# The first two rows of a macaron block: second row five chunks behind, its norm spread over chunks, weight tiles turned in other places, terms of h two chunks ahead

## The chip, the cores and the metric

The kernel runs on one core of a Trainium2 chip. The metric is the device time of one execution in microseconds; the time before is the median of three runs.

## The reference

Eight rows of 512 tokens with 512 channels go through a feed-forward layer, a sliding-window attention and a second feed-forward layer with the same weights. Only the first layer matters here. Its weights are quantised on the way in, to groups of 64 with one scale:

```
w = w_fp32.astype(bfloat16);  w_g = w.reshape(-1, 64)
scale = clip(mean(abs(w_g)), 1e-8)
w_hat = clip(round(w_g / scale), -1, 1) * scale
xn = layernorm(x)
gate, up = split(xn @ w_hat_gate_up.T)          # 2048 each
h = silu(gate) * up
x = x + 0.5 * (h * rsqrt(mean(h*h) + eps)) @ w_hat_proj.T
```

## The kernel before

A stage of the feed-forward layer (`ffn_stage`) handles one row (512 tokens) after the other. The 2048 hidden channels are cut into FC = 16 chunks of 128. For a chunk, TensorE (PE) makes gate and up with 8 matmuls each (`gate_or_up`), since x is held as a high and a low term over 4 blocks of channels; ScalarE (ACT) makes silu of gate; VectorE (DVE) multiplies it with up (`product`); ACT copies h as its high term (`high_term`), DVE makes the low term (`low_term`), and PE projects the chunk with 8 matmuls (`project`) into four accumulators, LAG = 2 chunks later. The sum of h squared per token, which scales the output at the end (`finish`), comes from a matmul with a column of ones.

The first two rows (`first_rows`) run together, because the weights are quantised while they are used. The order on PE, DVE and ACT is written out by hand; GpSimd (POOL) and the DMA queue of SP take their part where the dependencies let them. A `Quantised` tile is one chunk of gate and up weights (g, 16 of them) or two chunks of projection weights (pr, 8 of them). It goes through these steps: load (SP), magnitude and sign (ACT), scales (DVE), spread of the scales over the groups (ACT), five operations in two halves (DVE), and `turned`: eight PE transposes into PSUM, a copy by ACT into the weight tile, and a store of that tile for the last stage. The weight tile g[c+1] is quantised during chunk c.

In the loop over c, row 0 is at chunk c and row 1 at chunk d = c - LAG. Row 0 is normed ahead of the loop; the statistics of row 1 come all at the end of chunk 0, and its scaling and transposes (`normed`) all at the end of chunk 1. Row 1's h is squared, summed on DVE (sumsq) and stored in DRAM (h_kept), because PSUM holds the accumulators of one row only. After the loop it is loaded back (`back`), its terms are made again and it is projected, while the norm of row 2 runs between the chunks (`spread_norm`). The rest of the rows run one at a time.

What a PSUM pool holds matters for the order. Gate and up share two buffers: gate of one row takes the buffer that the gate before it left when its silu had been read, and up the one that the product before it freed. The transposes of the norm and of the weights share two buffers of `ps_tr`, and one of these holds the sums of squares of row 0 (`ms_first`) all along. The terms of h (hs) have three buffers, the pool `work` for silu, h, squares and back has five.

In one chunk before, PE issues gate and up of row 0, the turning of g[c+1], gate and up of row 1, the sums of row 0's squares, in even chunks the turning of pr[u-1], and the projection of chunk c - 2. ACT's order has magnitude and sign of g[c+2] ahead of silu of row 0, then the copy of the turned weights, the high term and the square.

Of the kernel before, what the change touches and what calls it, by code (L numbers as in the profile page):

```python
# [24 lines left out]
def macaron_block(  # L25
# [34 lines left out]
    nc.vector.tensor_copy(ident16, ident)  # L60
    ones = const.tile([P, 1], F32, name="ones")
    nc.vector.memset(ones, 1.0)
    mhalf = const.tile([P, TB], F32, name="mhalf")
    nc.vector.memset(mhalf, -0.5)

# [46 lines left out]
    class Quantised:  # L112
# [20 lines left out]
            self.wf = self.stage.tile(self.shape, F32, tag="wf", name=f"wf_{self.name}", bufs=2)  # L133
            nc.sync.dma_start(self.wf, self.src)

        def magnitude_and_sign(self):

            self.mag = self.bf16(f"mag_{self.kind}", self.ahead)
            nc.scalar.activation(self.mag, self.wf, AF.Abs)
            self.sgn = self.bf16(f"sgn_{self.kind}", self.ahead)  # L140
            nc.scalar.activation(self.sgn, self.wf, AF.Sign)

# [46 lines left out]


    def inv_sqrt(dst, src):
        nc.gpsimd.tensor_tensor(dst, src, mhalf, ALU.pow)

    def norm(xnpool, xspool, psum, tag, xt, split, name):

        if split:
            xs = xspool.tile([P, 2, DC, T], F32R, tag="xs", name=f"xs_{name}")
        else:  # L200
            xs = xspool.tile([P, DC, T], F32, tag="xs", name=f"xs_{name}")
        mv = small.tile([P, TB, 2], F32, tag="mv", name=f"mv_{name}")
        rstd = small.tile([P, TB], F32, tag="nrstd", name=f"rstd_{name}")

        def statistics(t):
            st = small.tile([P, 6], F32, tag="st", name=f"st_{name}_{t}")
            nc.vector.bn_stats(st, xt[:, t, :])
            nc.vector.bn_aggr(mv[:, t, :], st)
            if t == TB - 1:
                var = small.tile([P, TB], F32, tag="nvar", name=f"var_{name}")  # L210
                nc.vector.tensor_scalar(var, mv[:, :, 1], LN_EPS, None, ALU.add)
                inv_sqrt(rstd, var)

        xns = {}

        def scaled(t):
            xns[t] = xnpool.tile([P, D], F32, tag="xn", name=f"xn_{name}_{t}")
            nc.vector.tensor_scalar(
                xns[t], xt[:, t, :], mv[:, t, 0:1], rstd[:, t : t + 1], ALU.subtract, ALU.mult
            )  # L220

        def transposed(t):
            xn = xns.pop(t)
            pt = psum.tile([P, DC, P], F32, tag=tag, name=f"ptn_{name}_{t}")
            for c in range(DC):
                nc.tensor.transpose(pt[:, c, :], xn[:, c * P : (c + 1) * P], ident)  # L226
            cols = slice(t * P, (t + 1) * P)
            if split:
                nc.scalar.copy(xs[:, 0, :, cols], pt)  # L229
                nc.vector.tensor_tensor(  # L230
                    xs[:, 1, :, cols], pt, xs[:, 0, :, cols].bitcast(F32), ALU.subtract
                )
            else:
                nc.scalar.copy(xs[:, :, cols], pt)

        return xs, statistics, scaled, transposed


    LAG = 2

    def ffn_stage(kind, source, target, first):
# [26 lines left out]
        def row_loaded(b):  # L268
            xts[b] = xpool.tile([P, TB, D], F32, tag="x", name=f"x_{kind}{b}")
            for t in range(TB) if first and b == 0 else [slice(None)]:  # L270
                nc.sync.dma_start(xts[b][:, t], source(b)[:, t])
            xss[b], *norms[b] = norm(
                xnpool, xspools[b % 2], ps_tr, "tr", xts[b], True, f"{kind}{b}"
            )

        def gate_or_up(b, c, i):
# [12 lines left out]
        def silu(b, c, gate):  # L289
            sg = work_tile("sg", b, c)  # L290
            nc.scalar.activation(sg, gate, AF.Silu)  # L291
            return sg
# [11 lines left out]
        def low_term(h, hs):  # L304
            nc.vector.tensor_tensor(hs[:, 1, :], h, hs[:, 0, :].bitcast(F32), ALU.subtract)  # L305
# [6 lines left out]
        def project(ops, e, hs):  # L312
            for t in range(TB):
                for part in range(2):
                    nc.tensor.matmul(  # L315
                        ops[t], hs[:, part, t * P : (t + 1) * P], wp[e // 2][:, e % 2, :],
                        start=(e == 0 and part == 0), stop=(e == FC - 1 and part == 1),
                    )
# [36 lines left out]
        def first_rows():  # L355


            own = ExitStack()
            ms = ps_tr.tile([P, TB], F32, tag="tr", name="ms_first")
            stage = own.enter_context(tc.tile_pool(name="stage", bufs=1))  # L360
# [11 lines left out]
            waiting = list(order)  # L372

            def begun(tile_):
                tile_.magnitude_and_sign()
                if waiting:
                    waiting.pop(0).load()

            def normed(b, t):

                if t < TB:
                    norms[b][1](t)
                if t >= 1:
                    norms[b][2](t - 1)
# [22 lines left out]
            ops = outputs(0)  # L407
            sumsq = work.tile([P, T], F32, tag="ss", name="ss_second", bufs=1)
            hs, square = {}, None
            for c in range(FC + LAG):  # L410
                u, odd, d = c // 2, c % 2 == 1, c - LAG
                if c < FC:
                    gate0 = gate_or_up(0, c, 0)
                    up0 = gate_or_up(0, c, 1)
                    if c + 2 < FC:
                        begun(g[c + 2])
                    sg0 = silu(0, c, gate0)
                    if c + 1 < FC:
                        g[c + 1].first_half()
                        g[c + 1].second_half()  # L420
                    h0 = product(0, c, up0, sg0)
                    if c + 1 < FC:
                        g[c + 1].turned()
                    hs[c] = high_term(0, c, h0)
                    if odd:
                        pr[u].first_half()
                    else:
                        pr[u].scales()
                if c == FC + 1:
                    project(ops, d, hs.pop(d))  # L430
                if d >= 0:
                    gate1 = gate_or_up(1, d, 0)
                    up1 = gate_or_up(1, d, 1)
                if c < FC:
                    low_term(h0, hs[c])
                    sq0 = work_tile("sq", 0, c)
                    nc.scalar.activation(sq0, h0, AF.Square)
                    if c + 2 < FC:
                        g[c + 2].scales()
                if d >= 0:  # L440
                    sg1 = silu(1, d, gate1)
                if c < FC:
                    if not odd:
                        pr[u].spread()
                    if c + 2 < FC:
                        g[c + 2].spread()
                if c == FC + 1:
                    finish(0, ops, ms)
                if d >= 0:
                    h1 = product(1, d, up1, sg1)  # L450
                    nc.sync.dma_start(h_kept[d], h1)

                    square = sumsq if d == 0 else work_tile("sq", 1, d)
                    nc.scalar.activation(square, h1, AF.Square)
                if c < FC:
                    if odd:
                        pr[u].second_half()
                        if u + 1 < FC // 2:
                            begun(pr[u + 1])
                    for t in range(TB):  # L460
                        nc.tensor.matmul(
                            ms[:, t : t + 1], sq0[:, t * P : (t + 1) * P], ones,
                            start=(c == 0 and t == 0), stop=(c == FC - 1 and t == TB - 1),
                        )
                if c == 0:
                    for t in range(TB):
                        norms[1][0](t)
                if c == 1:
                    for t in range(TB + 1):
                        normed(1, t)  # L470
                if not odd and u:
                    pr[u - 1].turned()
                if 0 <= d < FC - 1:
                    project(ops, d, hs.pop(d))
                if d >= 1:
                    nc.vector.tensor_tensor(sumsq, sumsq, square, ALU.add)


            ms = sums_of(1, sumsq)
            ops = outputs(1)  # L480
            kept = {}
            for e in range(-2, FC):
                if e + 2 < FC:
                    kept[e + 2] = work_tile("back", 1, e + 2)
                    nc.sync.dma_start(kept[e + 2], h_kept[e + 2])
                if e >= 0:
                    ht = high_term(1, e, kept[e])
                    low_term(kept.pop(e), ht)
                    project(ops, e, ht)
                if e == 1:  # L490
                    stored(0)
                spread_norm(2, e, 2)
            finish(1, ops, ms)
            own.close()
# [370 lines left out]
```

## Time and profile before

| what | value |
|---|---|
| median of three runs | 2529.14 us (2523.03 to 2530.17) |
| profiled execution | 2521.33 us, span 2519.4 us |
| mean granted TensorE clock | 0.986 |
| PE busy | 2421.2 us, 96% of the span |
| DVE busy | 1323.8 us, 53% |
| ACT busy | 983.2 us, 39% |
| POOL busy | 908.9 us, 36% |
| first gate matmul of row 0, chunk 0 | 24.48 us |
| first projection of row 1 | 242.60 us |
| last projection matmul of row 1 | ends at 284.70 us |

The busy shares are means over the whole span. The change touches the first 285 us alone, so the numbers of that stage are what to read: the busy time by stretch, the timeline of a chunk, and on each line of it the idle time before an instruction, with the instruction that ended it. The span runs from the first to the last instruction; the profiled execution is 1.9 us longer than its span.

### The profile page before, as it was taken

What the parts mean: (1) busy time and instruction counts of PE and PEld (TensorE: products, weight loads), DVE (VectorE), ACT (ScalarE), POOL (GpSimd) and SP (SyncE); (2) the same over time, 40 slices, a digit from 0 to 9 for tenths busy, and PEclk for the clock granted to TensorE, in tenths of its full rate; (3) what the DMA queues carried; (4) which work ended last, traced back from release to release, by engine and by line L of the source; (5) the groups of instructions that cost most, each with busy time, mean ns of one, the idle gap of its engine ahead of it and who ended that gap; (6) DMA issues with size and microseconds to landing.
All of it is one profiled execution on the core that took longest, in us unless ns stands there. A gap on an engine that the chain in (4) does not pass through costs nothing.

```text
span 2519.4 us, 40507 instructions
## 1 busy us (share of the span) xinstructions
PE 2421.2 (96%) x16184; PEld 1772.3 (70%) x16184; DVE 1323.8 (53%) x3800; ACT 983.2 (39%) x1476; POOL 908.9 (36%) x775
## 2 busy tenths in 40 slices
PE   4998999999999999999999999997999999999998
PEld 3777788888888455555555555554688888888887
DVE  6785444444443566666666666665334444443442
ACT  5773222222222256555555555556222222222221
POOL 0000244445445133333333333333245444444444
PEclk8999999999999999999999999999999999999999
DMA  3443200000011100011010000022300000000000
GB/s 134 154 152 117 79 1 34 34 34 1 34 68 51 51 1 27 18 39 35 23 35 18 23 18 23 18 101 85 125 13 22 34 34 1 34 34 1 34 17 17
DMA packets 43564, 111.65 MB, mean 44 GB/s; under 512 B 3440, under 2 KB 7536, under 8 KB 40304
## 3 DMA queue, kind: packets, MB, share of 16 engines
q1 hardware_dynamic: 33392, 83.90, 9.4%
q10 hardware_dynamic: 9984, 25.17, 3.0%
q8 instruction: 127, 2.08, 0.4%
q14 instruction: 61, 0.50, 0.1%
HBM read 67.11 MB, written 41.94 MB: 43 GB/s over the span
## 4 chain that ended last, share of the span: by engine, by line
PE 89%; DVE 5%; ACT 3%; DMA 1%; issue 1%; POOL 0%; SPq 0%; POOLq 0%; DVEq 0%; ACTq 0%
PE gu_c L280 19%; PE gu_a L280 17%; PE o_c L315 9%; PE o_a L315 8%; PE sm L651 5%; PE sp L683 5%; PE wk L597 5%; PE av L719 5%; PE wq L597 4%; PE wo L597 4%; PE wv L597 4%; PE abT L737 1%; PE neg L669 1%; PE ptn_a L226 1%; PE ptn_b L226 1%
## 5 line engine op out<-in xcount | busy, mean ns | idle before, releaser
L280 PE MATMUL gu_a<-xs_a,wgu_a 128*128 128x512 f32 x2048 | 494.7, 395 | 1.8 <-ACT wgu_a L176 1.1
L280 PE MATMUL gu_c<-xs_c,wgu_c 128*128 128x512 f32 x2048 | 491.1, 393 | 0.7 <-ACT xs_c L229 0.7
L703 POOL TENSOR_SCALAR_AFFINE_SELECT pT<-pT 128x1024 f32<-128x1024 f32 x224 | 242.3, 1102 | 592.1 <-ACT pT L698 592.1
L280 PEld LDWEIGHTS gu_a<-xs_a,wgu_a 128*128 128x128 f32 x2048 | 385.5, 190 | 82.1 <-ACT wgu_a L176 1.4
L280 PEld LDWEIGHTS gu_c<-xs_c,wgu_c 128*128 128x128 f32 x2048 | 383.6, 189 | 80.0 <-ACT xs_c L229 0.9
L660 DVE CUSTOM_DVE_ANT_0 seen<-sm,window 128x256 f32<-128x256 f32 (+1 forms) x1024 | 331.2, 388 | 142.5 <-PE sm L651 142.0
L315 PE MATMUL o_a<-wp_a,hs_a 128*128 128x512 f32 x1024 | 257.1, 396 | 17.0 <-ACT wp_a L176 10.5
L315 PE MATMUL o_c<-wp_c,hs_c 128*128 128x512 f32 x1024 | 251.5, 389 | 0.0
L517 POOL TENSOR_TENSOR sq_c<-h_c 128x512 f32<-128x512 f32 x120 | 125.0, 1042 | 316.0 <-DVE h_c L296 302.5
L296 DVE TENSOR_TENSOR h_c<-gu_c,sg_c 128x512 f32<-128x512 f32 x128 | 88.3, 690 | 281.5 <-PE gu_c L280 280.2
L315 PEld LDWEIGHTS o_a<-wp_a,hs_a 128*128 128x128 f32 x1024 | 192.6, 190 | 60.7 <-ACT wp_a L176 11.9
L696 ACT ACTIVATE pT<-sp 128x512 f32<-128x512 f32 (+1 forms) x384 | 181.2, 547 | 127.7 <-PE sp L683 127.7
L698 ACT ACTIVATE pT<-pT 128x2048 f32<-128x2048 f32 (+1 forms) x128 | 217.3, 1698 | 8.4 <-DVE pT L692 4.4
L315 PEld LDWEIGHTS o_c<-wp_c,hs_c 128*128 128x128 f32 x1024 | 192.2, 188 | 39.9
L296 DVE TENSOR_TENSOR h_a<-gu_a,sg_a 128x512 f32<-128x512 f32 x128 | 88.3, 690 | 239.4 <-PE gu_a L280 233.8
L518 POOL TENSOR_TENSOR ss_c<-ss_c,sq_c 128x512 f32<-128x512 f32 x120 | 192.2, 1602 | 8.9
L291 ACT ACTIVATE sg_c<-gu_c 128x512 f32<-128x512 f32 x128 | 76.6, 599 | 265.1 <-PE gu_c L280 249.5
L301 ACT CAST hs_c<-h_c 128x512 fp32r<-128x512 f32 x128 | 79.4, 621 | 250.0 <-DVE h_c L296 250.0
L517 POOL TENSOR_TENSOR sq_a<-h_a 128x512 f32<-128x512 f32 x90 | 94.2, 1047 | 228.8 <-DVE h_a L296 218.8
L305 DVE TENSOR_TENSOR hs_c<-h_c,hs_c 128x512 fp32r<-128x512 f32 x128 | 124.0, 969 | 83.2 <-ACT hs_c L301 83.2
L291 ACT ACTIVATE sg_a<-gu_a 128x512 f32<-128x512 f32 x128 | 76.4, 597 | 228.3 <-PE gu_a L280 219.3
L651 PE MATMUL sm<-k,q 32*128 32x256 f32 (+1 forms) x2048 | 147.5, 375 | 2.5 <-DVE negs L660 2.0
(135 smaller groups left out, 3019.1 us busy)
## 6 DMA issues: line engine op xcount, KB each, us to landing
wf_gu<-w_gate_up_dram SPq DMA_DIRECT2D x16, 512.0 KB, 3.5
wgu_kept<-wgu_a SPq DMA_DIRECT2D x16, 512.0 KB, 2.6
rows_a<-x_a ACTq DMA_DIRECT2D x8, 1024.0 KB, 3.9
x_b<-rows_a SPq DMA_DIRECT2D x8, 1024.0 KB, 4.9
xr<-rows_a ACTq DMA_DIRECT2D x32, 256.0 KB, 3.1
rows_b<-xr SPq DMA_DIRECT2D x32, 256.0 KB, 2.4
x_c<-rows_b SPq DMA_DIRECT2D x8, 1024.0 KB, 4.8
wgu_c<-wgu_kept SPq DMA_DIRECT2D x16, 512.0 KB, 6.6
```

Source lines behind the costliest of these rows:

```text
L280: nc.tensor.matmul(ps, wgu[c][:, i * DC + k, :], xss[b][:, part, k, :], start=(k == 0 and part == 0), stop=(k == DC - 1 and part == 1),)
L291: nc.scalar.activation(sg, gate, AF.Silu)
L296: nc.vector.tensor_tensor(h, up, sg, ALU.mult)
L315: nc.tensor.matmul(ops[t], hs[:, part, t * P : (t + 1) * P], wp[e // 2][:, e % 2, :], start=(e == 0 and part == 0), stop=(e == FC - 1 and ...
L517: nc.gpsimd.tensor_tensor(sq, h, h, ALU.mult)
L518: nc.gpsimd.tensor_tensor(sumsq, sumsq, sq, ALU.add)
L597: nc.tensor.matmul(ps, lhs, rhs, start=(n == 0), stop=(n == len(pairs) - 1))
L651: nc.tensor.matmul(tiles[g][:, h, : n * P], qs[i][h][r, t * P : (t + 1) * P], ks[i][r, at], start=True, stop=True,)
L660: nc.vector.tensor_tensor_reduce(out=seen[:, : n * P], in0=tiles[g][:, h, : n * P], in1=window[:, (2 - n) * P :], scale=-1.0, scalar=3.4e3 ...
L696: nc.scalar.activation(under, tiles[g][:, :, : n * P], AF.Relu, scale=-1.0)
L698: nc.scalar.activation(seen, seen, AF.Exp, scale=-1.0)
L703: nc.gpsimd.affine_select(out=half, in_=half, compare_op=ALU.is_ge, fill=0.0, base=0, pattern=[[0, 2 * NG], [sign, P]], channel_multiplier ...
```

## The change

Row 1 runs `BEHIND = TB + 1` = 5 chunks behind row 0 instead of 2, so the loop has 21 turns instead of 18. The norm of row 1 is spread: one block of statistics in each of the chunks 0 to 3, each with its own power on POOL (`each=True`), and one block of scaling and transposes in each of the chunks 1 to 4. The turning of g[c+1] moves behind gate and up of row 1, that of pr[u-1] between gate and up of row 1. The sign of g[c+2] comes after the silu of row 0. The projection of row 0 stays two chunks behind. After the loop, the loads of h run four chunks ahead instead of two, both terms of h are made two chunks ahead of the projection, and the sums of row 1 (`sums_of`) come after its second projected chunk. One activation with Silu is put at the very start, so that its table is the first one loaded.

```
+    nc.scalar.activation(const.tile([P, 1], F32, name="begin"), ones, AF.Silu)
...
+            if each or t == TB - 1:
+                which = slice(t if each else 0, t + 1)
+                var = small.tile([P, TB], F32, tag="nvar", name=f"var_{name}_{t}")
+                nc.vector.tensor_scalar(var[:, which], mv[:, which, 1], LN_EPS, None, ALU.add)
+                inv_sqrt(rstd[:, which], var[:, which])
...
+            BEHIND = TB + 1
...
-            for c in range(FC + LAG):
-                u, odd, d = c // 2, c % 2 == 1, c - LAG
+            for c in range(FC + BEHIND):
+                u, odd, d = c // 2, c % 2 == 1, c - BEHIND
...
                     if c + 2 < FC:
-                        begun(g[c + 2])
+                        g[c + 2].magnitude()
                     sg0 = silu(0, c, gate0)
+                    if c + 2 < FC:
+                        signed(g[c + 2])
...
                     h0 = product(0, c, up0, sg0)
-                    if c + 1 < FC:
-                        g[c + 1].turned()
                     hs[c] = high_term(0, c, h0)
...
                 if d >= 0:
                     gate1 = gate_or_up(1, d, 0)
+                if not odd and 0 < u <= FC // 2:
+                    pr[u - 1].turned()
+                if d >= 0:
                     up1 = gate_or_up(1, d, 1)
                 if c < FC:
+                    if c + 1 < FC:
+                        g[c + 1].turned()
                     low_term(h0, hs[c])
                     sq0 = work_tile("sq", 0, c)
                     nc.scalar.activation(sq0, h0, AF.Square)
...
-                if c == 0:
-                    for t in range(TB):
-                        norms[1][0](t)
-                if c == 1:
-                    for t in range(TB + 1):
-                        normed(1, t)
-                if not odd and u:
-                    pr[u - 1].turned()
-                if 0 <= d < FC - 1:
-                    project(ops, d, hs.pop(d))
+                if c < TB:
+                    norms[1][0](c)
+                if 1 <= c <= TB:
+                    norms[1][1](c - 1)
+                    norms[1][2](c - 1)
+                if 0 <= c - LAG < FC:
+                    project(ops, c - LAG, hs.pop(c - LAG))
+                if c == FC + LAG:
+                    finish(0, ops, ms)
...
-            ms = sums_of(1, sumsq)
             ops = outputs(1)
-            kept = {}
-            for e in range(-2, FC):
-                if e + 2 < FC:
-                    kept[e + 2] = work_tile("back", 1, e + 2)
-                    nc.sync.dma_start(kept[e + 2], h_kept[e + 2])
+            kept, terms = {}, {}
+            for e in range(-4, FC):
+                if e + 4 < FC:
+                    kept[e + 4] = work_tile("back", 1, e + 4)
+                    nc.sync.dma_start(kept[e + 4], h_kept[e + 4])
+                if 0 <= e + 2 < FC:
+                    terms[e + 2] = high_term(1, e + 2, kept[e + 2])
+                    low_term(kept.pop(e + 2), terms[e + 2])
                 if e >= 0:
-                    ht = high_term(1, e, kept[e])
-                    low_term(kept.pop(e), ht)
-                    project(ops, e, ht)
+                    project(ops, e, terms.pop(e))
                 if e == 1:
                     stored(0)
+                    ms = sums_of(1, sumsq)
```

## The prediction

> **What bounds the kernel now.** I read the page first, then the busy time of each engine by stretch, then the timeline of the stretches that the change touches, and last the order in which the two built programs issue on each engine. That order is the same from row 2 on, so only the first 284 us can differ. From the page:
>
> ```profile
> span 2519.4 us, 40507 instructions
> ...
> PE   4998999999999999999999999997999999999998
> ...
> PEclk8999999999999999999999999999999999999999
> ```
>
> A digit is 63 us. PE is under 90% in four slices, and two of them, the first (4) and the fourth (8, 189 to 252 us), lie in the first rows: that is where PE stands idle. The stretches below follow the start of row 0's gate matmul by chunk (chunk 0 at 24.5, 1 at 34.0, 2 at 57.0, 5 at 95.2, 15 at 214.2), then row 1's second projection from 242.6 to 283.8. Columns: PE, PEld, DVE, ACT and POOL busy, granted clock, DMA share.
>
> ```profile
> 24.50:34.00 9.50, 6.69 (x33) 5.33 (x33) 6.22 (x10) 9.33 (x11) 0.00 (x0) 1.00 0.62 216
> 34.00:57.00 23.00, 12.10 (x51) 9.21 (x50) 17.21 (x32) 10.42 (x14) 1.38 (x1) 0.66 0.20 71
> 57.00:71.90 14.90, 13.63 (x67) 11.05 (x66) 11.95 (x18) 10.96 (x14) 0.00 (x0) 0.84 0.33 123
> ...
> 95.20:118.70 23.50, 21.91 (x121) 17.92 (x120) 18.94 (x30) 16.89 (x22) 0.00 (x0) 1.00 0.46 157
> ...
> 214.20:242.60 28.40, 22.91 (x114) 18.57 (x112) 11.53 (x20) 6.88 (x11) 1.01 (x1) 1.00 0.20 70
> 242.60:283.80 41.20, 35.37 (x145) 26.95 (x146) 18.44 (x34) 11.27 (x19) 2.39 (x2) 0.96 0.40 139
> ```
>
> Chunk 1 (34 to 57) loses 11 us of PE to row 1's norm, the second projection 6. A pair of full chunks (23.5 us) loses only 1.6: 0.36 before the even chunk's turning of its weights and 1.23 before its projection, which waits for the copy of wp. So there is little to win in the full chunks, and something at both ends. Two places of the timeline carry the argument. Chunk 1:
>
> ```profile
> 41.91 0.62 PE L175 MATMUL ptq_gu<-ident,q_wt_gu 128*128 128x128 bf16 x8 [2.40 <-DVE q_wt_gu L168]
> ...
> 42.56 1.01 ACT L176 CAST wgu_a<-ptq_gu 128x1024 fp32r<-128x1024 bf16 x1 [3.97 <-PE ptq_gu L175]
> ...
> 43.47 0.62 ACT L301 CAST hs_a<-h_a 128x512 fp32r<-128x512 f32 x1
> ...
> 43.99 0.63 ACT L437 ACTIVATE sq_a<-h_a 128x512 f32<-128x512 f32 x1
> ...
> 44.67 1.86 PE L461 MATMUL ms_first<-ones,sq_a 128*128 128x1 f32 x8 [2.15 <-ACT sq_a L437]
> ```
>
> Where no row-1 matmul stands between the turning (ptq_gu) and the sums (ms_first), PE waits until ACT has copied the turned weights and squared h. In full chunks gate and up of row 1 stand there and hide it. The second place is the second projection, one of its last four chunks:
>
> ```profile
> 273.25 0.49 PE L315 MATMUL o_a<-wp_a,hs_a 128*128 128x512 f32 x1 [1.19 <-ACT hs_a L301]
> ...
> 274.06 1.89 PE L315 MATMUL o_a<-wp_a,hs_a 128*128 128x512 f32 x7 [0.31 <-DVE hs_a L305]
> ```
>
> The terms of h are made in the chunk that uses them, behind the copy of the next row's norm, and PE waits for both.
>
> **What the Trainium skill says.** "TensorE: Matmul & The Clock Gate", section "What's actually happening": the PE clock falls to half after one idle window of a free-running 3.4 us and returns after a busy one. The trace agrees: the clock reads 0.50 from 164 to 167 us, and the projection there takes 3.59 instead of 2.11 us. That followed 2.65 us of ms_first, ptq_p and a wait, not a whole window of idleness. The same page's table (row on queue depth) has ScalarE and VectorE as strict FIFO; the trace agrees, as sq_a waits behind wgu_a at 42.56 above. "ScalarE: Activation LUTs", section "What ACT_TABLE_LOAD costs": about 1283 ns a load; the trace shows two in this stage, 1.28 us each (0.78 and 29.19).
>
> **The change part by part.** Times are of the profiled execution.
>
> 1. Start. The Silu table is loaded at 0.8 in place of the first set, so the load at 29.19 goes; up0 of chunk 0 ends at 29.8, so this frees 1.3 us of ACT but at most 0.7 of the path. DVE's seven small constant operations (7.84 to 8.57) now stand behind qsum of g[0] instead of in a wait: +0.7 to everything up to gate0 of chunk 0. Together 0: chunk 1 begins at 34.1.
>
> 2. Chunks 1 to 4, row 0 alone. Each now carries a quarter of row 1's norm. Statistics 0.95 and scaling 0.5 stand last on DVE, and PE meets the norm's transposes (ptn) before its projection and the next gate. The chain of one chunk is therefore serial. Odd: after up0, DVE does h 0.6, half of p 1.35, low term 0.6, scales 1.35, second half of p 1.95, statistics and scaling 1.45 = 7.3; then ptn 1.1 and projection. Even: h 0.7, hs 0.6, copy of wp 0.95, ptq_gu 0.6, copy of wgu 1.0, square 0.6, ms 0.9, ptn 1.0 and projection. One buffer of ps_tr is held by ms_first, so ptq_gu waits for the copy of wp, and that copy is on the path. After such gaps PE starts cold: gate and up take 5.4 (as at 34.0) or, after a cold projection of 3.4, about 4.3. Chunk by chunk: 14.1 (no projection yet), 15.1, 16.4, 13.3. Gate0 of chunk 5 then starts at 93.0 against 95.2, but row 1 is three chunks further behind. POOL's four powers of 1.0 to 1.4 us replace one; scaling uses the power of the chunk before, so they are hidden. The statistics hold up nothing else on DVE that is late, except xn, which is counted.
>
> 3. Chunks 5 to 14, both rows. PE now issues gate0, up0, gate1, (ptq_p), up1, ptq_gu, ms, projection. The wait for wp goes (ptq_p lies before up1: 1.8 us cover the copy) and the wait for q_wt goes. But sq0 stands on ACT behind the copy of wgu, which waits for ptq_gu, and ms follows ptq_gu at once. The lost time is 0.04 + 0.91 + 0.63 + 0.05 = 1.63 us in every chunk, from the rows above without hs. PE per odd chunk: 3.63 + 3.75 + 0.62 + 1.63 + 0.81 + 1.96 = 12.4; even with ptq_p 0.43: 12.8. A pair is 25.2 against 23.5. Nobody else is later: DVE's quantising of 3.4 us ends 0.5 to 3 us before ptq_gu, h0 comes 0.7 us before up1 needs its PSUM buffer, product h1 ends before the next up0. Loads and stores on SP keep their chunk, a store of h by three chunks later. Five pairs: 126. Clock drops: the stretch of ptq, wait and ms is 3.05 us, now in each chunk; before, seven of 2.65 us gave one drop of 1.5 us. I take two, +3, bounds 0 and 15. Chunk 15 starts at 93.0 + 126 + 3 = 222.0 against 214.2.
>
> 4. The end of row 1. Five chunks of row 1 are left instead of two. Chunk 15: 10.15, 16: 6.0, 17: 5.6, 18: 3.65. Then finish(0) lies on DVE between two products: h 0.7, var, POOL's power and half 1.6, four x_a 2.73, sum and h of chunk 14 1.3, so up1 of chunk 15 starts 6.35 after up1 of 13 and ends at 8.2 (0.9 late). From there to the first projection 4.5 as before (238.1 to 242.6: product, store issue 0.4, load of back 2.7, hs). 38.1 against 28.4; projection starts at 260.1 against 242.6.
>
> 5. Second projection. Before: 16 x 1.81 = 29.0, four transposes 2.4, cold start 1.6, one wait 0.6, and four chunks of 4.3 instead of 2.4 (7.6): 41.2. With terms two ahead the 7.6 goes: hs has three buffers, a term needs 1.4 us and has 3.6. ms (0.8) moves in from before it. rows_a is now issued behind hs of chunk 3, so x of row 2 lands some 14 us after the first projection (6.3 + 5.5 us as before) and DVE's statistics, with two low terms behind them, hold PE about 0.5. SP issues the load ahead of back 10 and later, which is early enough. Sum 34.3; the stage ends at 294.4.
>
> Against 283.8 (284.7 less 0.9 of gate work that PE had done early) this is **+10.6 us**. The profiled execution took 2521.3 (span 2519.4 and 1.9 around it), which gives 2531.9. The median of the runs shown, 2529.1, lies 7.8 above that execution, so I put the change on the median: 2539.7. Some 0.3%, 7.6 us, is about what a measurement of this kernel can tell from no change.
>
> **Rivals.**
> Faster: chunks 1 to 4 run at DVE's busy time, not at the serial chain. DVE has 11.4 us in an odd and 9.4 in an even one, so 10.3 on average; the four take 41 instead of 59, and with no clock drop the sum is 10.6 - 18 - 3 = -10: 2519 to 2521. For it: chunk 0 took 9.5. Against it: chunk 0 has no ptn and no projection. It decides if chunks 1 to 4 average below 10.5 us.
> Even: PE is warm there (4 us less) and no clock drops in full chunks (3 less): +3.6, 2533. For it: six of seven stretches before kept the clock.
> Slower still: each wait of 1.63 drops the clock: ten times 1.5 instead of 3, +22, 2552.
> The terms ahead do nothing, since hs buffers free too late: +7.6, 2547. Against it, the ring: a buffer is free two projections before it is needed.
>
> **How the numbers follow.** Forecast 0.48, even 0.26, faster 0.12, slower still 0.09, no gain in the terms 0.05. The forecast's own range is 2532 to 2548 (clock 0 to 4 drops, early chunks 5 either way); the whole one reaches to both edges, 2521 to 2552. Faster 0.12, same 0.27, slower 0.61.
>
> **What would show it.** Right: ms_first waiting about 1.6 us for sq_a some fifteen times; full pairs at 25.2; gate0 of chunk 5 near 93 and of chunk 15 near 222; the projections after 260 with no wait for hs_a. Wrong: pairs at or below 23.5, chunks 1 to 4 at 10 us, or a second projection near 41.

## The result and the profile after

The kernel after takes 2546.91 us (median of five runs, 2542.35 to 2548.10) against 2523.67 us of the kernel before on the same chip: a ratio of 1.0082, with a 95% interval of 1.0061 to 1.0103. It is slower by 23 us; the forecast was slower by 10.6. Its profiled execution took 2547.95 us with a span of 2546.1 us, that of before 2521.33 and 2519.4 us. From the page of after:

```profile
span 2546.1 us, 40511 instructions
...
PE   4889999999999999999999999998899999999998
...
PEclk9889999999999999999999999999899999999999
```

The second and the third slice (64 to 191 us) are now 8 in both rows, where before they were 9. They lie mostly in the full chunks, where the kernel before lost little. (The 8s further on are in code that the change doesn't touch.) The busy time by stretch says it in microseconds. The columns are the stretch, its length, busy time of PE, PE's weight loads, DVE, ACT and POOL, the granted clock, and the DMA share with GB/s. The stretches are chunks 1 to 4, chunks 5 to 14, the tail (from gate of row 0, chunk 15, to the first projection of row 1) and the second projection:

```profile
35.80:95.40 59.60, 40.47 (x186) 33.21 (x186) 42.62 (x74) 34.14 (x42) 2.89 (x4) 0.74 0.30 111
95.40:234.60 139.20, 122.89 (x602) 98.98 (x601) 90.75 (x140) 81.51 (x106) 0.00 (x0) 0.90 0.34 121
234.60:272.80 38.20, 32.78 (x153) 26.46 (x151) 15.46 (x25) 10.47 (x17) 1.01 (x1) 1.00 0.20 72
272.80:306.50 33.70, 33.65 (x152) 27.55 (x153) 18.64 (x34) 11.47 (x19) 1.57 (x2) 0.95 0.52 168
```

Against before:

| stretch | before | forecast | after |
|---|---|---|---|
| gate0 of chunk 1 starts | 34.0 | 34.1 | 35.8 |
| chunks 1 to 4 | 61.2 | 58.9 | 59.6 |
| chunks 5 to 14 | 119.0 | 129 | 139.1 |
| tail | 28.4 | 38.1 | 38.3 |
| second projection | 41.2 | 34.3 | 33.7 |
| end of the first rows | 283.8 | 294.4 | 306.6 |

In chunks 5 to 14 PE is idle for 16 us, which is ten waits of 1.63, and the clock is 0.90 where before it was 0.99. The waits of PE in the first rows (total, times, longest):

```profile
PE ms_first L474 <- ACT sq_a L452: 26.6, 15, 2.5
...
PE o_a L322 <- ACT hs_a L308: 4.7, 1, 4.7
...
PE gu_a L287 <- DVE h_a L303: 0.7, 1, 0.7
```

One full chunk of after in the timeline (start, duration, what, and in brackets the idle time before it with what ended it):

```profile
184.92 0.62 PE L179 MATMUL ptq_gu<-ident,q_wt_gu 128*128 128x128 bf16 x8
...
185.58 1.01 ACT L180 CAST wgu_a<-ptq_gu 128x1024 fp32r<-128x1024 bf16 x1 [2.67 <-PE ptq_gu L179]
186.49 0.63 ACT L452 ACTIVATE sq_a<-h_a 128x512 f32<-128x512 f32 x1
...
187.17 1.54 PE L474 MATMUL ms_first<-ones,sq_a 128*128 128x1 f32 x8 [1.63 <-ACT sq_a L452]
...
188.58 3.76 PE L322 MATMUL o_a<-wp_a,hs_a 128*128 128x512 f32 x8
```

The square of h stands on ACT behind the copy of the turned weights (186.49 behind 185.58), ms_first waits 1.63 us for it, and the projection behind it runs at half clock: 3.76 us, where a chunk that kept the clock shows 2.10. Seven of the ten chunks lost it. The rest of the span is 2239.5 us against 2235.6. Its instructions are the same, and in the profiled executions of all the kernels below it lies between 2234 and 2240 us, so these 3.9 us are no more than executions differ by and are not put down to the change.

### The profile page after: what moved, and what is told of

Its sections match the earlier page's. It is cut to its first block, busy times and chain, and to the rows that moved or that the text cites. A ratio compares the mean times of both kernels' runs of the same rounds, so it can differ in the third digit from the quotient of the medians.

```text
span 2546.1 us, 40511 instructions
## 1 busy us (share of the span) xinstructions
PE 2440.0 (96%) x16184; PEld 1788.0 (70%) x16184; DVE 1324.2 (52%) x3803; ACT 983.5 (39%) x1476; POOL 909.2 (36%) x778
## 4 chain that ended last, share of the span: by engine, by line
PE 92%; DVE 3%; ACT 2%; DMA 1%; issue 1%; POOL 0%; SPq 0%; POOLq 0%; DVEq 0%; ACTq 0%
PE gu_c L287 18%; PE gu_a L287 18%; PE o_a L322 10%; PE o_c L322 9%; PE sm L665 5%; PE sp L697 5%; PE wk L611 5%; PE av L733 4%; PE wq L611 4%; PE wo L611 4%; PE wv L611 4%; PE abT L751 1%; PE neg L683 1%; PE ptn_a L232 1%; PE ptn_b L232 1%
## 5 line engine op out<-in xcount | busy, mean ns | idle before, releaser
L322 PE MATMUL o_a<-wp_a,hs_a 128*128 128x512 f32 x1024 | 269.4, 410 | 4.7 <-ACT hs_a L308 4.7
L322 PEld LDWEIGHTS o_a<-wp_a,hs_a 128*128 128x128 f32 x1024 | 201.6, 199 | 47.9 <-ACT hs_a L308 5.2
L308 ACT CAST hs_a<-h_a 128x512 fp32r<-128x512 f32 x112 | 69.5, 621 | 210.9 <-DVE h_a L303 210.9
```

The lines of the kernel that those rows point to most:

```text
L308: nc.scalar.copy(hs[:, 0, :], h)
L322: nc.tensor.matmul(ops[t], hs[:, part, t * P : (t + 1) * P], wp[e // 2][:, e % 2, :], start=(e == 0 and part == 0), stop=(e == FC - 1 and ...
```

## The experiments

Theory 1 was that the full chunks lose, through the wait of ms_first and the drops that come with it. Theory 2 was that the lag loses: four serial chunks ahead of row 1, and row 1 alone at the end. All were timed against the kernel before on their own chip. Stretches are of one execution of each kernel, the profiled one; "drops" counts how often the clock was halved in chunks 5 to 14.

| kernel | ratio to before (95%) | chunks 1-4 | chunks 5-14 | drops | tail | second projection |
|---|---|---|---|---|---|---|
| before | 1 | 61.2 | 119.0 | 1 | 28.4 | 41.2 |
| after | 1.0082 (1.0061-1.0103) | 59.6 | 139.1 | 7 | 38.3 | 33.7 |
| 1 turning put back | 0.9981 (0.9971-0.9991) | 59.6 | 112.9 | 0 | 38.2 | 35.1 |
| 2 square first | 0.9965 (0.9953-0.9977) | 58.9 | 113.9 | 0 | 38.3 | 34.8 |
| 3 terms alone | 0.9970 (0.9960-0.9979) | 59.5 | 119.0 | 1 | 30.0 | 34.3 |
| 4 turning alone | 1.0192 (1.0173-1.0210) | 71.5 | 155.2 | all 10 | 29.4 | 40.4 |
| 5 lag two | 0.9948 (0.9933-0.9963) | 58.6 | 117.2 | 0 | 26.6 | 34.6 |
| 6 sums last | 1.0000 (0.9991-1.0010) | 60.3 | 117.7 | 0 | 38.3 | 33.9 |
| 7 loads early | 0.9928 (0.9912-0.9945) | 58.4 | 117.2 | 0 | 21.5 | 34.4 |
| 8 sign late | 0.9912 (0.9898-0.9926) | 57.5 | 114.5 | 0 | 21.5 | 34.6 |
| 9 sign early | 1.0092 (1.0078-1.0107) | 59.2 | 142.4 | 8 | 38.3 | 33.7 |
| 10 square between | 1.0093 (1.0077-1.0109) | 60.2 | 136.6 | 9 | 38.3 | 34.9 |
| 11 after, longer | 1.0065 (1.0047-1.0084) | 59.8 | 140.8 | 2 | 39.3 | 34.0 |
| 12 between, longer | 1.0064 (1.0046-1.0082) | 59.4 | 136.2 | 3 | 38.6 | 35.2 |

### 1 and 2: the wait taken away in two ways

The turning put back where before had it:

```
+                    if c + 1 < FC:
+                        g[c + 1].turned()
                     hs[c] = high_term(0, c, h0)
...
-                    if c + 1 < FC:
-                        g[c + 1].turned()
                     low_term(h0, hs[c])
```

> The kernel after with the turning of g[c+1] alone put back where the kernel before has it, between gate and up of row 0 and of row 1. Theory 1 (the full chunks lose by ms_first waiting behind the copy of wgu, and by the clock drops that this stretch brings): the wait of 1.63 us is gone in chunks 5 to 14, a pair takes about 22.4 us instead of 27.8, chunks 5 to 14 about 112 to 115 us instead of 139.1, clock there 0.98 or more; the kernel at 2518 to 2523 us, no slower than before. Theory 2 (the lag of five chunks is the loss, with four serial chunks ahead and row 1 alone at the end): still 2538 or more.

One ACT instruction moved:

```
                     hs[c] = high_term(0, c, h0)
+                    sq0 = work_tile("sq", 0, c)
+                    nc.scalar.activation(sq0, h0, AF.Square)
...
                     low_term(h0, hs[c])
-                    sq0 = work_tile("sq", 0, c)
-                    nc.scalar.activation(sq0, h0, AF.Square)
```

> The kernel after with one ACT instruction moved: the square of h of row 0 comes right behind the high term, ahead of the copies of wp and wgu. PE's order stays. Theory 1: ms_first no longer waits (at most 0.2 us), PE goes from ptq_gu to ms_first to the projection without a gap, pairs take about 22 us, chunks 5 to 14 about 110 to 115 us, few clock drops; 2515 to 2522 us. Theory 2: within 5 us of the kernel after. If the short matmuls of ms_first and the transposes themselves, not the wait, let the clock drop: the wait goes (16 us gained) and the drops stay at about seven of ten (10 us not gained), about 2530 us.

Measured: 2520.10 and 2515.69 us against 2525.06. Both undo the loss of the full chunks, 112.9 and 113.9 us, with no drop. PE in the run with the square first:

```profile
189.30 2.11 PE L287 MATMUL gu_a<-xs_a,wgu_a 128*128 128x512 f32 x8 [0.49 <-DVE h_a L303]
191.24 0.62 PE L179 MATMUL ptq_gu<-ident,q_wt_gu 128*128 128x128 bf16 x8
191.70 1.00 PE L474 MATMUL ms_first<-ones,sq_a 128*128 128x1 f32 x8
192.57 2.10 PE L322 MATMUL o_a<-wp_a,hs_a 128*128 128x512 f32 x8
```

ms_first follows ptq_gu at once and the projection is warm. The ten chunks take 25 us less than in after, with PE's order unchanged. ACT has room for the square there: in after it stands idle for 2.67 us ahead of the copy (185.58 above). The place of one ACT instruction was thus worth more than the 23 us that the whole change lost, and both of these kernels are faster than before with the lag of five chunks in them. The third case (that the short matmuls and transposes alone let the clock drop) is out as well: they are still there, and no full chunk lost the clock.

### 3 and 4: one part of the change put into the kernel before

```
+                if e + 4 < FC:
...
+                if 0 <= e + 2 < FC:
+                    terms[e + 2] = high_term(1, e + 2, kept[e + 2])
+                    low_term(kept.pop(e + 2), terms[e + 2])
```

> The kernel before with the second projection of the kernel after alone: loads four ahead, both terms two chunks ahead, sums after the second chunk. If the terms ahead take away the waits for hs_a: the second projection takes about 34 us instead of 41.2, the kernel 6 to 8 us faster than before, about 2516 to 2518 us. If they are hidden anyway or the buffers of hs come free too late: no difference.

Measured: 2518.50 against 2525.06 us; the second projection takes 34.3 us instead of 41.2. The terms ahead are worth what was forecast, without the rest of the change. (The tail is 1.6 us longer than before; one halving of the clock, from 231.7 us on, falls into it.)

```
-                    if c + 1 < FC:
-                        g[c + 1].turned()
                     hs[c] = high_term(0, c, h0)
...
+                    if c + 1 < FC:
+                        g[c + 1].turned()
                     low_term(h0, hs[c])
```

> The kernel before with the turning of g[c+1] alone moved behind gate and up of row 1, as the kernel after has it; the lag stays two chunks. Theory 1: ms_first waits 1.63 us in every full chunk, some seven in ten of the full chunks lose 1.4 us more to the halved clock, the wait for wp stays: 12 chunks x 1.6 + 8 x 1.4 = 30 us less what waits now overlap, +20 to +30 us, 2543 to 2553 us. Theory 2: within 5 us of the kernel before.

Measured: 2573.28 us, 48 more than before, beyond the expectation of 20 to 30. Chunks 5 to 14:

```profile
106.30:261.60 155.30, 130.71 (x602) 105.50 (x601) 89.95 (x138) 80.08 (x105) 0.00 (x0) 0.84 0.30 108
```

Of the 48 us, 36 are in these chunks and 10 in chunks 1 to 4. PE is idle for 24.6 of 155.3 us and the clock is at 0.84: every one of the ten chunks lost it, and in even chunks the wait for wp stays behind ms_first (1.3 to 2.3 us) and keeps the clock low for longer. The kernel after, which turns pr[u-1] between gate and up of row 1, has no such wait in its full chunks.

### 5: the lag taken away

Kernel before with the square first, the two turnings as in after, and the terms ahead; lag and norm of row 1 as before. From the run with the square first it differs by more than the lag and the spread norm: the sign of g[c+2] is early, and the activation at the start is missing.

```
                     gate1 = gate_or_up(1, d, 0)
+                if not odd and u:
+                    pr[u - 1].turned()
+                if d >= 0:
                     up1 = gate_or_up(1, d, 1)
```

> The kernel before, with its lag of two chunks and its norm of row 1 in chunks 0 and 1, and with everything of the kernel after that the runs so far showed to pay or to be free once the square is early: square of h right behind the high term, g[c+1] turned behind row 1's gate and up, pr[u-1] turned between them, second projection with terms two ahead. It differs from the run with the square first by the lag and the spread norm alone. Theory 2 in its remaining form (the lag moves 3 x 3.6 us of PE work of row 1 from stretches where PE idles anyway to the end, where it adds up): chunks 1 to 4 about 60 us, 5 to 14 about 113, tail about 28.4 instead of 38.3, second projection 34.5; 7 to 9 us faster than the run with the square first, about 2507 to 2510 us. Rival (the spread norm earns back in chunks 1 to 4 what the tail costs): within 2 us of the run with the square first, 2514 to 2518.

Measured: 2510.66 against 2523.86 us. The tail shrinks from 38.3 to 26.6 us, and chunks 1 to 4 take 58.6 us, no more than with the lag of five (58.9). So the lag, with the spread norm that goes with it, buys nothing ahead and costs 11.7 us at the end: theory 2 holds for this share. The full chunks, though, take 117.2 us and not 113, for a wait for silu (sg_a) that the run with the square first does not have (waits of PE in chunks 5 to 14):

```profile
PE gu_a L280 <- ACT sg_a L291: 3.7, 4, 0.9
PE gu_a L280 <- DVE h_a L296: 1.3, 6, 0.2
```

The total is 5 us below that of the run with the square first, less than the 7 to 9 expected, and since the two intervals overlap, the total alone would not separate them; that the tail is shorter is read from the stretches.

### 6: the sums behind the projection

```
                 if 0 <= c - LAG < FC:
                     project(ops, c - LAG, hs.pop(c - LAG))
+                if c < FC:
+                    for t in range(TB):
+                        nc.tensor.matmul(
+                            ms[:, t : t + 1], sq0[:, t * P : (t + 1) * P], ones,
```

> The kernel after with ACT's order untouched (square behind the copy of wgu) and ms_first moved on PE alone, behind the projection. The 2.1 us of projection now cover the 1.63 us that the square is late. If the place of ms_first on PE is what lets the wait show, and the gap is what drops the clock: no wait, projection warm at 2.1 us in all ten chunks, pairs about 22.5 us, within 3 us of the run with the square first, 2513 to 2519 us. If ACT's order is itself what is late (silu of row 1, the copies): the wait shows up elsewhere and the time stays above 2530.

Measured: 2525.17 against 2523.86 us, not the 2513 to 2519 expected. The wait and the drops went as expected (117.7 us, clock 1.00), so ACT's order costs this much only because ms_first followed ptq_gu at once on PE. But 3.8 us of the gain came back in other waits (4.6 us in all for h and 1.8 for silu, against 2.1 and none in the run with the square first), and the start and chunks 1 to 4 took 4 us more than in that run:

```profile
149.25 2.11 PE L287 MATMUL gu_a<-xs_a,wgu_a 128*128 128x512 f32 x8 [0.96 <-DVE h_a L303]
...
151.63 2.08 PE L322 MATMUL o_a<-wp_a,hs_a 128*128 128x512 f32 x8
```

up of row 1 now waits 0.96 us for the product h of row 0, where the run with the square first shows 0.49. I read this as the chain of ACT and DVE, in which the square is still late, setting the pace in PE's place; no run tests it.

### 7 and 8: what the runs pointed to

In all kernels up to here PE stands idle ahead of the second projection and then starts it cold. In after:

```profile
265.99 2.12 PE L287 MATMUL gu_a<-xs_a,wgu_a 128*128 128x512 f32 x8 [0.72 <-DVE h_a L303]
272.85 4.32 PE L322 MATMUL o_a<-wp_a,hs_a 128*128 128x512 f32 x10 [4.75 <-ACT hs_a L308]
```

The load of back 0 is issued behind the store of the last h, though what it loads was stored long before.

```
+                    terms[0] = high_term(1, 0, kept[0])
+                    low_term(kept.pop(0), terms[0])
...
+                if c == FC:
+                    for e in range(2):
+                        kept[e] = work_tile("back", 1, e)
+                        nc.sync.dma_start(kept[e], h_kept[e])
```

> The lag-two kernel of this set, and the loads of back 0 and 1 and the terms of back 0 moved into the loop: the loads into the turn of chunk 14 of row 1, the terms ahead of the last product. In all kernels so far PE waits 4.7 us for hs_a at the start of the second projection and then starts at half clock (6.2 us for 16 matmuls instead of 3.8). If this wait is the load issued behind the last store: both go, second projection starts right after the last up, 6 to 7 us faster than the lag-two kernel, about 2501 to 2504 us. If the ring of work buffers or the accumulators of row 0 hold it: 0 to 2 us.

Measured: 2504.79 us, 5.9 below the lag-two kernel, just short of the 6 to 7 expected; the tail falls from 26.6 to 21.5 us. The projection follows up without a gap and warm:

```profile
228.29 3.79 PE L280 MATMUL gu_a<-xs_a,wgu_a 128*128 128x512 f32 x16
231.91 2.66 PE L315 MATMUL o_a<-wp_a,hs_a 128*128 128x512 f32 x9
```

To this the late sign of the change was added:

```
-                        begun(g[c + 2])
+                        g[c + 2].magnitude()
                     sg0 = silu(0, c, gate0)
+                    if c + 2 < FC:
+                        signed(g[c + 2])
```

> The lag-two kernel with the early loads, and the sign of g[c+2] behind the silu of row 0, as the kernel after has it: the one part of the change that the runs so far have not looked at. In the lag-two kernels PE waits 0.91 us for sg_a before gate of row 1 in even full chunks, 0.22 us for h_a in odd ones; in the run with the square first (sign late) only 0.47 for h_a in odd ones. If the sign ahead of silu is what makes silu late: the wait of 0.91 goes, pairs fall from 23.5 to about 22.8 us, chunks 5 to 14 from 117 to about 114 us, the kernel 3 to 4 us faster, about 2501 us. If the silu waits for gate0 itself: no difference.

Measured: 2500.09 us against 2522.46, ratio 0.9912: the fastest kernel here by its median, faster than before and after. Its interval overlaps that of run 7; the gain over run 7 is read from the stretches: the wait for sg_a is gone and the ten chunks take 114.4 us instead of 117.2. Chunks 5 to 14 and the tail:

```profile
91.20:205.60 114.40, 111.80 (x601) 88.84 (x600) 92.34 (x143) 81.83 (x109) 0.00 (x0) 1.00 0.39 147
205.60:227.10 21.50, 21.50 (x106) 17.74 (x104) 11.25 (x19) 6.56 (x11) 1.01 (x1) 1.00 0.26 97
```

### 9: the sign alone put back in after

```
-                        g[c + 2].magnitude()
+                        begun(g[c + 2])
                     sg0 = silu(0, c, gate0)
-                    if c + 2 < FC:
-                        signed(g[c + 2])
```

> The kernel after with the sign of g[c+2] alone put back ahead of the silu of row 0. If the late sign pays in the kernel after as well: a wait of about 0.9 us for sg_a at gate of row 1 in even chunks, +4 to +6 us against the kernel after, about 2551 to 2553 us. If the wait for sq_a takes it in (PE arrives later, and ms_first then waits less): within 2 us of 2547. Either way ms_first still waits for sq_a, and most full chunks lose the clock.

Measured: 2544.28 us, ratio 1.0092: no different from after. PE has no wait for sg_a there; I take it that PE comes too late to meet it. The late sign showed a gain only where the wait of ms_first was gone (run 8).

### 10, 11 and 12: what decides the number of drops

```
+                nc.scalar.copy(self.dst[:, :half, :], pt[:, :half, :])
+                between()
+                nc.scalar.copy(self.dst[:, half:, :], pt[:, half:, :])
```

> The kernel after with the copy of the turned gate and up weights by ACT in two halves and the square of h of row 0 between them; PE's order and everything else stay. The wait of ms_first for sq_a becomes about 1.15 us instead of 1.63, and the stretch without long matmuls (ptq_gu, wait, ms_first) about 2.55 us instead of 3.05. The step that the prediction mis-sized is the number of clock drops; this run asks what decides it. If the length of the stretch decides (3.05 us: seven and eight drops of ten; 2.65 us before: one of seven; 1.6 us: none of twenty): one to three drops in chunks 5 to 14, these about 139 - 5 (waits) - 7 (drops) = 127 us, the kernel at 2533 to 2537 us. If any wait in this place drops the clock: about seven drops, 134 us, 2541 to 2543 us.

Measured: the wait is 1.20 us and ptq_gu to projection 2.74 us:

```profile
184.84 0.62 PE L179 MATMUL ptq_gu<-ident,q_wt_gu 128*128 128x128 bf16 x8
186.66 1.05 PE L481 MATMUL ms_first<-ones,sq_a 128*128 128x1 f32 x8 [1.20 <-ACT sq_a L456]
187.58 3.15 PE L328 MATMUL o_a<-wp_a,hs_a 128*128 128x512 f32 x8
```

That is nearly the 2.65 of before, where one stretch in seven lost the clock. Here nine of ten chunks did, and the kernel took 2543.68 us, not the 2533 to 2537 expected if the length decides. So the length of the stretch alone does not decide. Stretches of this kernel, cut where the clock changes:

```profile
188.30:191.70 3.40, 3.40 (x9) 2.66 (x9) 3.33 (x7) 3.40 (x5) 0.00 (x0) 0.51 0.47 184
191.70:201.90 10.20, 8.99 (x55) 7.21 (x55) 6.55 (x11) 5.70 (x10) 0.00 (x0) 1.00 0.43 154
201.90:205.30 3.40, 3.40 (x9) 2.63 (x9) 1.69 (x3) 3.11 (x4) 0.00 (x0) 0.51 0.61 233
...
215.60:219.00 3.40, 3.40 (x10) 2.64 (x9) 3.37 (x6) 2.94 (x4) 0.00 (x0) 0.51 0.56 219
```

The half clock lasts 3.4 us and begins at 188.3, 201.9 and then 215.6, that is, every 13.65 us or 4 steps of 3.413. The nine drops of this run all begin on this grid, the second eight steps after the first and each of the others four steps after the one before. In the traces of all fourteen kernels the clock changes only on such a grid, to within 4 ns over the whole span, and its place against the first instruction differs from trace to trace (0.15 to 3.32 us). A chunk that keeps the clock takes some 12.1 us, 3.6 steps (run 12 has a pair of 26.25 us with 1.96 of added work in it). Where each chunk loses it, it is 13.8 us from one gap to the next (145.5 to 228.4 us, six chunks), 4.05 steps, and so the next gap meets nearly the same phase. To test this, work without use was added, which moves the phase (again is 2 for gate of row 1 in chunks 5 to 14):

```
+            for k in range(again):
+                for part in range(2):
+                    nc.tensor.matmul(
+                        ps, wgu[c][:, i * DC + k, :], xss[b][:, part, k, :],
+                        start=(k == 0 and part == 0), stop=(k == again - 1 and part == 1),
+                    )
```

> The kernel after with PE work added that does nothing for the result: in chunks 5 to 14 the first 4 of the 8 matmuls of gate of row 1 are issued twice (4 x 0.245 = 0.98 us a chunk, 9.8 us in all); the second pass overwrites the first. The gap with ptq_gu, the wait of 1.63 and ms_first stays. In the traces so far clock drops begin only on a grid of 3.41 us, and those of the kernel with the square between lie exactly 13.64 us = 4 grid steps apart, chunk after chunk: a chunk of 12 us without a drop (3.5 steps) becomes one of 13.6 with it, and so the next gap meets the same phase of the grid. Theory (the drops lock to the grid): with 1 us more a chunk is 13.4 us or, with a drop, some 14.9 (4.4 steps), so a drop is not followed by the next: 1 to 4 drops of ten instead of seven, chunks 5 to 14 at 139 + 9.8 - 4 to 8 = 141 to 145 us, the kernel 2 to 6 us slower than the kernel after. Rival (the gap drops the clock by its length, whatever the phase): seven drops, 149 us, 10 us slower, 2557.

> The same 4 matmuls added to the kernel with the square between the halves of the copy, where nine of ten chunks lost the clock in lock step. Theory (lock): chunks of 13.0 us without and 14.5 with a drop (3.8 and 4.25 steps): 0 to 3 drops, chunks 5 to 14 at 136.6 + 9.8 - 9 to 13 = 133 to 138 us: 9.8 us of useless work cost next to nothing, 2540 to 2546 us. Rival (length of the gap alone): nine drops, 146 us, 2553.

Measured: 2543.56 us (ratio 1.0065) and 2542.49 us (1.0064): with 9.8 us more work neither is slower than the kernel it was added to (2 to 6 us more was expected of run 11). Drops fall from seven to two (of two windows each) and from nine to three. The mean clock, which every timed execution has, goes the same way: 0.977 to 0.980 in five of after, 0.980 to 0.986 in six of run 11; 0.975 to 0.976 in run 10, 0.980 to 0.983 in run 12. In run 11 the clock holds through eight chunks, waits of 1.63 us and all:

```profile
96.70:215.90 119.20, 104.52 (x560) 84.90 (x559) 80.12 (x124) 72.39 (x95) 0.00 (x0) 1.00 0.35 124
```

The rival, that the gap drops the clock by its length (146 to 149 us for the ten chunks, 2553 to 2557 in all), is out: the ten chunks took 136.2 and 140.8 us. Run 11 also shows the other side of the lock. A chunk that keeps the clock there takes 13.55 us, 3.97 steps, so the gap stays for long where it does no harm and creeps 0.1 us a chunk. In the window with the gap, the matmuls of 512 columns run for 1.81, 1.96, 1.57, 1.76, 1.37, 1.56, 1.17 and 1.36 us in chunks 5 to 12, and the clock stays; in chunk 13 they run for 0.97 us, and it falls. It falls again in chunk 14, so "a drop is not followed by the next" did not hold there.

## Why the prediction was right in direction and short in size

1. Start: forecast +0.1 at gate0 of chunk 1, seen +1.8. Of the 0.7 for DVE's constants 0.5 is there: from qsum of g[0] to the first scaling it is 1.85 us in each of the eight kernels with the early activation of Silu and 1.34 in each of the six without it. Another 0.8 is no part of the change: the first weights landed later in this execution, so their magnitude started at 8.92 us instead of 8.13 (7.79 to 9.09 in the fourteen, with the load issued at 2.62 to 2.64 in all). The up to 0.7 credited for the table load does not show: chunk 0 takes 8.6 to 11.4 us with it and 8.7 to 10.8 without. The remaining 0.5 is within that spread.
2. Chunks 1 to 4: forecast 58.9, seen 59.6, with the single chunks at 13.0, 15.6, 15.9 and 15.2 where 14.1, 15.1, 16.4 and 13.3 were forecast. The serial chain is right, and the copy of wp is on it (two waits of 1.95); that the sum is off by 0.7 only is in part luck, since the first chunk was put 1.1 too long and the last 1.9 too short.
3. **Full chunks: the step that failed is "I take two".** The wait is 1.63 us in each of the ten, as forecast, and a pair that keeps its clock is right too: in run 11 four pairs without a drop take 27.1 us each, of which 1.96 is the added work, which leaves 25.1 (forecast 25.2). So the ten chunks would be 126, and some 13 us of the 139.1 are seven drops of 1.9 each, where the sum had two of 1.5. The rate of before (one in seven) was carried over as if each gap were a fresh draw; runs 10 to 12 show that the phase of the gap decides, and that in chunks of this length a drop brings the next gap near the same phase. The upper bound of 15 held it.
4. Tail: 38.1 forecast, 38.3 seen; up1 of chunk 15 is 0.72 late for DVE's h_a (forecast 0.9).
5. Second projection: 34.3 forecast, 33.7 seen, no wait for hs_a but the first. Run 3 shows it by itself. (The sum of 34.3 also leaves out the 0.6 of the one wait, which the text of the prediction does not say.)

The differences add up: 1.7 + 0.7 + 10.1 + 0.2 - 0.6 = 12.1, of the 12.2 between 294.4 and 306.6. The rival of drops in all ten chunks was nearest in mechanism, the faster rival (chunks 1 to 4 below 10.5 us) failed at its own point, and "no gain in the terms", whose 2547 is the measured time, is refuted by run 3: its number was luck. Luck helped the forecast too. The forecast was put on the median of 2529.14 us; measured again beside the kernel after, the kernel before took 2523.67. So 2546.91 lies within the forecast's 2532 to 2548, though the loss of 23 us is more than the 19 at the end of that range. What the prediction left out was the remedy: the wait was put down to the turning, and that one ACT instruction could be issued ahead of the copy at no cost came only with the runs.

The Trainium skill, "TensorE: Matmul & The Clock Gate", section "What's actually happening", gives a free-running window of about 3.4 us; here the spacing of 13.65 us agrees with its 3413 ns times four. It lets the clock fall after an idle window. Here it also fell after windows that were not idle. Between 95 and 235 us the fourteen traces have 522 windows at full clock, 42 of them followed by the half clock. Added up from the records, matmuls of 512 columns ran for at most 0.97 us in 38 of these 42, and for 1.02 us or more in all of the other 480. The remaining four (1.08 to 1.42 us) fall into line when each window is counted 0.2 to 0.4 us earlier than the record has it (at 0.3: at most 1.27 us, against 1.32 or more). With the transposes and ms_first counted in, the two kinds overlap. Where the limit lies is read off, not tested by itself.

## What to carry to other kernels

When instructions are moved on one in-order engine, look on every other engine for what now stands ahead of the operand that the next instruction needs; here the answer was to issue one square ahead of a copy. A gap in a loop on PE is not priced by its own length: compute the loop's period in clock windows with and without a drop, since a period near a whole number of windows brings each gap to the phase of the last, with the drop (run 10: 4.05) or without it (run 11: 3.97). A part of a change that shows nothing (the late sign) may be worth some 3 us when the wait that covers it is gone, so parts are tried again after the main loss is mended.

## What the hardware showed that I had not expected

The half clock comes in whole steps of 3.41 us on a grid that the kernel does not set, so the cost of a gap can hang on its phase: 1.20 us of wait with nine drops (136.6 us) cost nearly as much as 1.63 us with seven (139.1 us). And useless matmuls can be free: 9.8 us of them in each of runs 11 and 12 left the time where it was or below.
